# Turning a residual during attention: three generator steps for each block of x instead of two

## The chip, the core and the metric

The kernel runs on one core of a Trainium2 chip. The metric is the device time of one execution in microseconds, as the median of several runs. TensorE is called PE here, VectorE DVE, ScalarE ACT, GpSimd POOL and SyncE SP.

## What is computed

Two layers of the same kind follow each other. Each normalises x in groups of channels, runs attention with 12 heads of 64 channels over 48 x 48 positions, with relative positions added to the scores, projects the result and adds it to x. Cut to what matters:

```
x = x + attention0(group_norm(x))
x = x + attention1(group_norm(x))

attention(x):                                   # x: 2304 positions, 768 channels
    q, k, v = x @ qkv_w + qkv_b                 # layer 0 adds a low-rank term to q and v
    attn = softmax(q * scale @ k.T + rel_h + rel_w)
    return (attn @ v) @ proj_w + proj_b
```

## The kernel before

**Stages.** A layer runs `group_norm`, `project` (keys and values), `project_q` (queries and relative positions), `attend` and `out_project`. Keys, values, queries and relative positions go through DRAM between the stages. x is kept with channels on the partitions, in six blocks of 384 positions (QB); its residual lies in DRAM in that form, as `residuals`. The last projection puts out rows of positions, so in layer 1 the residual has to be turned from channels by positions to positions by channels (`res_tokens`) ahead of it.

**Attention** (`attend_plain`, L864 to L1082). The work is cut into 30 blocks, one pair of heads and up to 512 queries each (L873): five blocks to a pair, of 512, 512, 512, 512 and 256 queries. I call the last a short block. A block goes through 18 tiles of 128 keys in two batches of nine. For each tile PE makes the scores in PSUM (ps_sc, three buffers), ACT their exponentials (pt, L981), DVE adds these up (L987). The values of a batch (ps_ov) are multiplied one batch later, in `catch_up`. So the end of block n lies in block n+1: its denominators (ps_d, L1013) with their reciprocal (L1021) when the second batch of block n is worked off, then the product for o on DVE (L1025), its bias on ACT (L1026), and the stores of o (f_o, L1030) and of the reciprocals (f_rec, L1032), which POOL issues.

**What sets the order.** Instructions given to `in_order` (L158) keep their order in the program on their engine; all PE work of attention does, and so does everything in `turn`. The others are placed by the framework's planner. Each engine runs its queue from the front: an instruction that waits holds all behind it. SP issues the loads of keys (L899), values (L908), queries (L932) and relative positions (L942, L946). POOL issues the stores and all transfers of `turn`.

**Work beside attention.** `attend` gets a generator, `beside` (L1287), and steps it once at the end of each block but the first, 29 times:

```
                if i > 0:
                    next(beside, None)
```

In layer 0 the generator loads the weights of the projection and adds up their four sums (`sums_of_a`, L401: one DVE addition or subtraction to a step, L412). In layer 1 it first runs `turn`:

```
                if li == 1:
                    yield from turn(residuals[1], res_tokens, p3, bt)
                w_all = p3.tile([P, CT, C], F32, tag="w", name="wproj")
```

`turn` (L1216 to L1241) takes the six blocks of x one by one. For each it loads the block (POOL, L1223), adds the projection's bias with six ACT activations (L1226), transposes squares of 32 x 32 with one DVE instruction (L1231), and stores the result with 24 transfers from POOL (L1238). The tile of a block holds the loaded and the turned half, and there is one buffer for it (tag "w"), which the weights of the projection use too. So each load, and that of the weights (L1293) at the end, waits until the stores before it have landed. A block of x takes two steps: a `yield` stands behind its load, and another behind the third of the six activations. There is none at the end of the loop, so the stores of a block and the load of the next one come in the same step: steps 1 to 12 are used, the weights are loaded at step 13, and their sums follow at steps 14 to 17.

Of the kernel before, what the change touches and what calls it, by code (L numbers as in the profile page):

```python
# [55 lines left out]
def two_layers(tc: tile.TileContext, x, layers, out):  # L56


    nc = tc.nc
    with tc.tile_pool(name="verdict", bufs=1) as vp:  # L60
        bad = vp.tile([1, 1], mybir.dt.int32, tag="bad", name="bad")
        compute(tc, x, layers, out, "f", bad)
        again = nc.values_load(
            bad, min_val=0, max_val=1,
            skip_runtime_bounds_check_because="the result of a comparison",
        )
        with tc.If(again > 0):
            compute(tc, x, layers, out, "g", None)
# [3 lines left out]
def compute(ctx: ExitStack, tc: tile.TileContext, x, layers, out, run, bad):  # L72
# [38 lines left out]
    def scratch(name, shape):  # L111
        name = f"{run}_{name}"
        return dram.tile(shape, F32, tag=name, name=name)
# [44 lines left out]
    def in_order(instruction):  # L158

        tc.keep_in_program_order(instruction)  # L160
# [1055 lines left out]
    def turn(res, to, pool, bt):  # L1216


        for b in range(NQB):

            both = pool.tile([P, 2, CT, QB], F32, tag="w", name=f"x_turned_{b}")
            x, turned = both[:, 0], both[:, 1]
            in_order(nc.gpsimd.dma_start(x, res[b]))  # L1223
            yield
            for t in range(CT):
                in_order(nc.scalar.activation(  # L1226
                    x[:, t], x[:, t], AF.Identity, bias=bt[:, t : t + 1]
                ))
                if t == HP - 1:
                    yield  # L1230
            in_order(nc.vector.transpose(  # L1231
                turned.rearrange("p t q -> p (t q)"), x.rearrange("p t q -> p (t q)")
            ))
            rows = to[ts(b, QB), :].rearrange("(f i) c -> i f c", i=32)
            for t in range(CT):
                for r in range(P // 32):
                    lo = t * P + r * 32
                    in_order(nc.gpsimd.dma_start(  # L1238
                        rows[:, :, lo : lo + 32],
                        turned[ts(r, 32), t].rearrange("p (f j) -> p f j", j=32),  # L1240
                    ))  # L1241

    residuals = [[scratch(f"res{li}_{b}", [P, CT, QB]) for b in range(NQB)] for li in range(2)]
    res_tokens = scratch("res_tokens", [N, C])
# [16 lines left out]
    for li, ly in enumerate(layers):  # L1261
# [21 lines left out]
        with tc.tile_pool(name="p3_w", bufs=1, **REUSE) as p3:  # L1283
# [3 lines left out]
            def beside(li=li, ly=ly, p3=p3, bt=bt, w=w):  # L1287
                in_order(nc.gpsimd.dma_start(bt, ly.proj_bt))
# [3 lines that stand above are left out]
                s = p3.tile([P, 3, HP, HP * P], F32, tag="s", name="wproj_s")  # L1292
                in_order(nc.gpsimd.dma_start(w_all, ly.proj_w.rearrange("(t p) n -> p t n", p=P)))  # L1293
                factors, steps = sums_of_a(
                    matrix_blocks(w_all, HP * P), *(s[:, i] for i in range(3))
                )
                w.update(factors)
                yield
                yield from steps
# [95 lines left out]
```

## Time and profile before

| | us |
|---|---|
| median of 3 runs | 3280.67 |
| lowest and highest run | 3269.58 and 3292.76 |
| the profiled execution | 3272.56 |
| its span, from the first instruction to the last | 3270.8 |
| x_turned <- f_res, one load of x, 1152 KB: issue to landing, median | 5.8 |
| f_res_tokens <- x_turned, one of 24 stores, 48 KB: issue to landing, median | 2.4 |
| wproj <- in_proj_w, the weights' load, 2304 KB: issue to landing, median of both layers | 13.6 |

The profile is of one execution. Its page gives the busy time of each engine and the costliest groups of instructions; the timelines give instructions in order of time. A row of a timeline has the start in us from the span's start, the duration in us of all that it holds, engine, line, operation, tiles (out <- in), shapes, count, and, in brackets, how long the engine was idle before it and what ended that. The median of the runs is 8.1 us above the profiled execution, so sums are made on the profile's span and carried over to the median as a difference.

### The profile page before, as it was taken

Reading aid. Unit: us, or ns where it says so; the run is one execution under the profiler, and the core shown is the slowest. Engines: PE = TensorE matmul, PEld = TensorE weight load, DVE = VectorE, ACT = ScalarE, POOL = GpSimd, SP = SyncE. Lnnn points to the kernel's source line nnn. Section 1 sums busy time; section 2 is a strip of 40 time slices with the busy share of each in tenths; the row PEclk is TensorE's granted clock in tenths of the full one; section 3 lists DMA queues with packets and bytes.
Section 4 is the critical chain, followed back from the end, with each engine's and each line's share of the span. In section 5 each row is a group of like instructions: output and inputs, shape, how many; then the busy total and the mean of one; then the engine's idle time right before and its main releaser. Section 6 shows DMA issues by size and latency. Waiting matters only on the chain. (4 is left out here: it accounts for less than half of the span.)

```text
span 3270.8 us, 50009 instructions
## 1 busy us (share of the span) xinstructions
PE 3209.8 (98%) x19600; PEld 1995.9 (61%) x19600; DVE 2112.6 (65%) x2281; ACT 1450.0 (44%) x1673; POOL 468.4 (14%) x855
## 2 busy tenths in 40 slices
PE   8999999999999999999989999999999999999999
PEld 5555666665656665656555566656666656656555
DVE  8432437777777777777774234576778767777764
ACT  3101436555555555653011024655566555555520
POOL 2144110000000000000012531102223200000000
PEclk9999999999999999999999999999999999999999
DMA  7333388353536262724234335766556463435251
GB/s 267 130 82 74 130 261 219 82 128 78 133 74 142 67 152 64 153 62 160 101 126 145 58 106 197 240 137 145 123 136 149 117 147 79 127 78 135 66 205 59
DMA packets 225155, 419.76 MB, mean 128 GB/s; under 512 B 43616, under 2 KB 111104, under 8 KB 221072
## 3 DMA queue, kind: packets, MB, share of 16 engines
q1 hardware_dynamic: 177712, 255.35, 31.8%
q0 software_dynamic: 47200, 161.12, 16.1%
q8 instruction: 158, 2.59, 0.3%
q14 instruction: 85, 0.70, 0.1%
HBM read 260.35 MB, written 155.97 MB: 127 GB/s over the span
## 5 line engine op out<-in xcount | busy, mean ns | idle before, releaser
L987 DVE TENSOR_TENSOR sum<-sum,pt 128x1024 f32<-128x1024 f32 (+1 forms) x960 | 1071.1, 1116 | 187.9 <-ACT pt L981 97.0
L954 PE MATMUL ps_sc<-q,k 64*128 64x512 f32 (+1 forms) x8640 | 1085.6, 371 | 13.9 <-ACT pt L981 12.3
L981 ACT ACTIVATE pt<-ps_sc 128x1024 f32<-128x1024 f32 (+1 forms) x1080 | 1009.8, 941 | 174.4 <-PE ps_sc L954 89.0
L954 PEld LDWEIGHTS ps_sc<-q,k 64*128 64x128 f32 x8640 | 782.2, 185 | 226.0 <-issue 46.0
L954 PE MATMUL ps_ov<-pt,v 128*64 128x512 f32 (+1 forms) x4320 | 857.7, 551 | 0.0
L954 PEld LDWEIGHTS ps_ov<-pt,v 128*64 128x64 f32 x4320 | 301.2, 137 | 497.6 <-issue 443.3
L954 PE MATMUL ps_sc<-rel,places 64*128 64x512 f32 (+1 forms) x2160 | 413.6, 371 | 1.9 <-DMA rel<-f_r 1.6
L1032 POOL DMA_DIRECT2D f_rec<-rec x120 | 58.5, 492 | 1588.5 <-DVE rec L1021 1587.1
L698 PE MATMUL ps_q<-xT,w_q 128*128 128x384 f32 x864 | 285.1, 488 | 0.7 <-DVE v L587 0.7
L1026 ACT ACTIVATE o<-o,v_bias 128x512 f32<-128x512 f32 (+1 forms) x60 | 40.9, 681 | 459.2 <-DVE o L1025 453.6
L954 PEld LDWEIGHTS ps_sc<-rel,places 64*128 64x128 f32 x2160 | 211.7, 185 | 33.4 <-issue 2.6
L698 PEld LDWEIGHTS ps_q<-xT,w_q 128*128 128x128 f32 x864 | 163.0, 191 | 110.1 <-issue 2.5
L1021 DVE RECIPROCAL rec<-ps_d 128x512 f32<-128x512 f32 (+1 forms) x60 | 181.9, 3031 | 2.5 <-PE ps_d L954 2.5
L601 POOL DMA_DIRECT2D f_v<-v x288 | 137.3, 485 | 106.4 <-DVE v L587 101.5
L987 DVE TENSOR_TENSOR sum<-pt 128x1024 f32<-128x1024 f32 (+1 forms) x60 | 67.0, 1117 | 128.9 <-ACT pt L981 128.9
L523 PE MATMUL ps_k<-xt,w_k 128*128 128x384 f32 x432 | 145.1, 492 | 3.6 <-DVE xt L427 2.6
L704 DVE TENSOR_SCALAR x_q<-ps_q,bt 128x384 f32<-128x384 f32 x72 | 44.3, 617 | 159.5 <-PE ps_q L698 159.5
L996 ACT CAST sum<-sum 128x1024 bf16<-128x1024 f32 (+1 forms) x60 | 57.6, 960 | 168.1 <-DVE sum L987 168.1
L523 PEld LDWEIGHTS ps_k<-xt,w_k 128*128 128x128 f32 x432 | 82.3, 192 | 63.9 <-issue 3.6
L523 PE MATMUL ps_k<-xT,w_k 128*128 128x384 f32 x324 | 114.6, 507 | 4.7 <-DVE xT L249 4.6
L999 DVE TENSOR_TENSOR sum<-sum,sum 128x1024 bf16<-128x1024 f32 (+1 forms) x60 | 67.1, 1119 | 61.6 <-ACT sum L998 61.6
L997 DVE TENSOR_TENSOR sum<-sum,sum 128x1024 f32<-128x1024 f32 (+1 forms) x60 | 67.1, 1119 | 61.6 <-ACT sum L996 61.6
(183 smaller groups left out, 2474.7 us busy)
## 6 DMA issues: line engine op xcount, KB each, us to landing
rel<-f_r SPq DMA_DIRECT2D x1152, 96.0 KB, 4.3
f_k<-xs POOLq DMA_DIRECT2D x72, 384.0 KB, 2.9
f_q<-xs_q POOLq DMA_DIRECT2D x48, 576.0 KB, 3.8
k<-f_k SPq DMA_DIRECT2D x48, 576.0 KB, 5.2
q<-f_q SPq DMA_DIRECT2D x96, 256.0 KB, 3.2
f_r<-relh POOLq DMA_DIRECT2D x48, 432.0 KB, 5.0
f_r<-relw POOLq DMA_DIRECT2D x8, 2592.0 KB, 18.1
f_v<-v POOLq DMA_DIRECT2D x288, 48.0 KB, 2.0
```

The lines of the kernel that those rows point to most:

```text
L523: nc.tensor.matmul(ps, lhsT=x, rhs=y, start=(t == 0), stop=(t == HP - 1))
L601: nc.gpsimd.dma_start(vd[to : to + KG, :], v[ts(r, KG), k])
L698: nc.tensor.matmul(ps, lhsT=w[:, t, ts(pr, P)], rhs=xT[b][:, t, :], start=(t == 0), stop=(t == CT - 1),)
L704: nc.vector.tensor_scalar(x[:, pr], ps, weights.bt[:, pair : pair + 1], ly.q_scale, ALU.add, ALU.mult,)
L954: in_order(nc.tensor.matmul(*args, **kwargs))
L981: nc.scalar.activation(pt, ps[:, :, 0 : self.n], AF.Exp)
L987: nc.vector.tensor_add(self.sum, self.first if kt == 1 else self.sum, pt)
L996: nc.scalar.copy(hi, self.sum)
L997: nc.vector.tensor_sub(self.sum, self.sum, hi)
L999: nc.vector.tensor_sub(lo, self.sum, mid)
L1021: nc.vector.reciprocal(self.rec, ps)
L1032: nc.gpsimd.dma_start(recs[li][2 * self.pair + r : 2 * self.pair + r + 1, to], self.rec[r * HD : r * HD + 1, :],)
```

## The change

A `yield` is put at the end of the loop over the blocks of x in `turn`:

```diff
@@ -1239,6 +1239,7 @@
                         rows[:, :, lo : lo + 32],
                         turned[ts(r, 32), t].rearrange("p (f j) -> p f j", j=32),
                     ))
+            yield
 
     residuals = [[scratch(f"res{li}_{b}", [P, CT, QB]) for b in range(NQB)] for li in range(2)]
     res_tokens = scratch("res_tokens", [N, C])
```

A block of x now takes three steps: its load; three of its six activations; and the other three, the transpose and the stores. The load of the next block is the step after that. With b from 0 to 5 these are steps 3b+1, 3b+2 and 3b+3. The weights' load becomes step 19, and their sums steps 20 to 23. No instruction is added or left out, and layer 0 doesn't run `turn`. A second version of the computation in the same program (`attend_shifted`), which runs only if a value is out of bounds, runs the generator through at once.

## The prediction

> **What bounds the kernel now.** I read the page first, for the engine that sets the time, then each stage of the second layer's attention by the busy times of chosen windows, then the timelines of the engines in the stages that are too long.
>
> ```profile
> span 3270.8 us, 50009 instructions
> PE 3209.8 (98%) x19600; PEld 1995.9 (61%) x19600; DVE 2112.6 (65%) x2281; ACT 1450.0 (44%) x1673; POOL 468.4 (14%) x855
> ```
>
> TensorE (PE) sets the time: whatever does not stop it costs nothing. The turn of x runs on ACT, DVE and POOL, so its price is only the time in which PE stands still because of it. The windows show where (start and end, length, PE busy; PEclk is the granted TensorE clock):
>
> ```profile
> core 0: us, PE busy (x) PEld busy (x) DVE busy (x) ACT busy (x) POOL busy (x), PEclk, DMA share, GB/s
> 2252.00:2288.00 36.00, 31.88 (x276) 21.55 (x274) 22.95 (x26) 17.83 (x26) 15.42 (x26) 0.95 0.89 230
> 2428.00:2458.00 30.00, 29.57 (x266) 19.60 (x266) 22.16 (x23) 17.22 (x26) 6.49 (x12) 1.00 0.62 172
> 2628.00:2671.00 43.00, 35.12 (x260) 24.75 (x262) 34.01 (x29) 20.73 (x21) 1.56 (x3) 0.92 0.78 153
> 2671.00:2778.00 107.00, 107.00 (x771) 62.88 (x772) 79.81 (x64) 59.78 (x63) 4.65 (x9) 1.00 0.34 76
> ```
>
> PE is idle for 4.1, 0.4 and 7.9 us in three places, and the clock is below 1.00 in two of them; in the last row, after the turn, it never stops. To price the places I measure from the first denominator matmul (ps_d) of one block to that of the next, in PE's timeline. Without a disturbance a pair of heads has the intervals 37.47, 37.47, 32.49, 28.95 and 33.32 us (every pair of layer 0, and the last of layer 1). I number layer 1's blocks from 0; blocks 4, 9, 14, ... are the short ones (256 queries). Interval n runs from ps_d of block n to that of block n+1. Longer than they should be are: interval 3, 35.04 (6.09 too many); 8 and 9, 29.63 and 33.74 (0.68 and 0.42); 14, 43.05 (9.73). Together 16.9 us: this is all that the turn and the load of the weights cost, and all that can be won.
>
> **The first place** (PE, then ACT, then POOL):
>
> ```profile
> 2274.34 0.41 PE L954 MATMUL ps_sc<-rel,places 64*128 64x512 f32 x2
> 2278.82 2.07 PE L954 MATMUL ps_sc<-q,k 64*128 64x512 f32 x8 [4.07 <-ACT pt L981]
> 2280.69 0.63 PE L954 MATMUL ps_sc<-rel,places 64*128 64x512 f32 x2
> 2281.12 1.49 PE L954 MATMUL ps_sc<-q,k 64*128 64x512 f32 x8
> ```
> ```profile
> 2271.41 0.62 ACT L998 CAST sum<-sum 128x512 bf16<-128x512 f32 x1 [0.76 <-DVE sum L997]
> 2276.23 1.62 ACT L1226 ACTIVATE x_turned<-x_turned,bproj 128x384 f32<-128x384 f32 x3 [4.21 <-DMA x_turned<-f_res]
> ```
> ```profile
> 2257.05 9.72 POOL L1238 DMA_DIRECT2D f_res_tokens<-x_turned  x16 [1.47 <-DMA f_res_tokens<-x_turned]
> 2266.76 0.57 POOL L1030 DMA_DIRECT2D f_o<-o  x1
> 2267.33 0.99 POOL L1032 DMA_DIRECT2D f_rec<-rec  x2
> 2268.79 0.57 POOL L1223 DMA_DIRECT2D x_turned<-f_res  x1 [0.47 <-issue]
> ```
>
> Read from below: POOL issues the 24 stores of x block 0 into short block 4, and the load of x block 1, which takes the same buffer, leaves only at 2268.79. It lands 7.1 us later. Block 4 lasts too short: ACT comes to the bias of x block 1 at 2272.0 and waits 4.21 us. Behind it in ACT's queue stand the exponentials of block 5, so the three PSUM buffers of the scores stay full and PE stops for 4.07 us. Then 8 score matmuls take 2.07 us instead of 1.09: the slow clock is the other 2.02 of the 6.09 (0.05 of the window's 36 us is 1.8).
>
> **The second place** (DVE, ACT, PE):
>
> ```profile
> 2628.81 1.36 DVE L412 TENSOR_TENSOR wproj_s<-wproj 128x1152 f32<-128x1152 f32 x1 [9.46 <-DMA wproj<-in_proj_w_dram]
> ```
> ```profile
> 2642.39 0.51 ACT L1026 ACTIVATE o<-o,v_bias 128x256 f32<-128x256 f32 x1 [13.29 <-DVE o L1025]
> ```
> ```profile
> 2643.86 2.08 PE L954 MATMUL ps_sc<-q,k 64*128 64x512 f32 x8 [7.88 <-ACT pt L981]
> ```
>
> The same pattern: the stores of x block 5 go into short block 14, the load of the projection's weights leaves behind them at 2616.35 and takes 12.4 us. DVE wants to add two blocks of them at 2619.35, and waits 9.46 us with the sums and the product for o queued behind; ACT's bias of o waits for that product, with the exponentials behind it, and PE stands for 7.88 us. With the slow clock after it: 9.73.
>
> **The change, part by part.** The generator is stepped once at the end of each block from block 1 on. Before, step 2b+2 is the first half of the bias of x block b, and step 2b+3 is the second half, the transpose, the 24 stores and the next load. Now step 3b+2 is the first half, 3b+3 ends with the stores, and 3b+4 is the next load. Nothing is added to any engine: the same 36 biases, 6 transposes, 144 stores and 6 loads. [...]
>
> The load itself hardly moves: at short block 4 it was already put behind the f_o and f_rec of block 3, and waits for the same stores. What moves is its reader, one block later.
>
> 1. Bias of x block 1: from the end of block 4 (2272.0) to the end of block 5, 33.3 us on (the length of a pair's first block). The load landed at 2275.9, so it is 29 us early. Interval 3 falls to 28.95: **-6.09**.
> 2. Sum of the weights: from the end of block 14 to the end of block 20. The stores of x block 5 now go into short block 19, which is as short as 14, so I put the weight load as far from its start as before: landing some 11.4 us into block 20, 24 us before DVE asks (2.0 us after that block's 33.3). Interval 14 falls to 33.32: **-9.73**.
> 3. Step 9, after a short block, is second half and transpose as before (now of x block 2): its 1.10 us stay, **0**.
> 4. Step 14, after a short block, is now the first half of the bias of x block 4. The trace has no such step there without a wait. From below it costs 0, from above the 1.63 us of its three activations; the nearest row is step 9, the same three activations at the same place, 1.10 us. I take **+1.1**. Its load doesn't wait: x block 1 was loaded 18.1 us after its stores began (2314.04 to 2332.15) and a load takes 5.8 (median of the page), while step 14 comes some 58 us after the stores of step 12 begin.
> 5. All other steps lie at the ends of long blocks, or go into short ones (3, 8, 13 before; 3, 8, 18, 23 now). Their cover is the slack of ACT and DVE beside PE: 37.47 and 32.49 us with them as without. **0**; without that cover 1.6 us for a half bias and 2.6 for a transpose.
> 6. Queues: POOL has f_rec and f_o behind each set of stores as before (14.6 us), and intervals 5 and 7, where that was so, are not longer. On SP nothing is moved, but PE now comes earlier to what SP loads while the stores and the weights take the DMA engines. In block 15, whose place block 20 takes, the second half of the keys landed at 2620.7 and the values at 2630.7. With no stop PE wants them at 2632.0 and 2642.5 (block begun at 2617.4, 10.55 us per batch of scores, 4.04 for values): 11 us to spare for each. **0**.
>
> Sum: -6.09 - 9.73 + 1.1 = -14.7 us on a span of 3270.8: 3256.1. The profiled execution took 3272.6, 8.1 below the median of the runs (3280.67); on that median the sum gives **3266.0**.
>
> **A rule against it.** The Trainium skill, "DMA: Bandwidth & Descriptors", section "Anatomy of one DMA — SWDGE (gpsimd) path", fits a GpSimd-issued transfer as 2.0 us and its bytes at 436 GB/s. That is 4.7 us for the x load (1.18 MB) and 7.4 for the weights (2.36 MB), estimates from that page. The rows say 7.1 and 12.4, beside a DMA share of 0.78 to 0.89. By the rule ACT would wait 1.5 us and DVE 4.4, PE some 1.4 and 2.8, with at most the slow clock of now (2.0 and 1.9): 4.2 to 8.1 us to win, less the 1.1 of item 4, so 3273.7 to 3277.6. I take the rows, since they are the transfers in question.
>
> **Rivals.** *Both waits go* (0.72): 3266.0; for it speaks that both rows name their transfer as the releaser. *Only the first goes* (0.13): the weights' transfer, with SP's loads behind it in block 20, holds PE there as it did in block 15; against it stand the 11 us. -6.1 + 1.1: 3275.7. *Nothing comes of it* (0.09): the planner puts the readers where they were, or the run-to-run spread (3269.6 to 3292.8) is made of other things that grow: 3280.7. *Slower* (0.06): the planner, which places instructions outside the kept order itself, puts SP's loads of keys and queries later once the steps have moved, and PE waits at block boundaries. One such stop costs 6.1 to 9.7 us, as the two above; with two or three of them the gain is gone, and with eight (8 x 6.1 - 14.7 = +34) it is slower by 1%. Nothing in the trace shows such a wait: PE's largest stop for a DMA in this stage is 0.6 us.
>
> **Range and chances.** The likeliest case with the spread of the runs (-11 and +12) gives 3255 to 3278. Below, the fastest run less all 16.9 is 3253; above, the case of no gain is 3281. I say 3250 to 3284. 1%, about what a measurement of this kernel can tell from no change, is 33 us, about twice all that can be won here. Faster by that takes a lucky set of runs, 0.05; slower takes half of the last case, 0.03; within 1%, 0.92.
>
> **What would show it.** Right: no bias of x_turned that waits for its load, no sum of the weights that waits for theirs, intervals 3 and 14 at 28.95 and 33.32 us, interval 13 and 14 together up by about 1, PEclk 1.00 throughout. Wrong: a new stop in block 15 or 20, or ps_sc released by a DMA.

## The result, and the profile after

The changed kernel takes 3258.02 us (median of 13 runs, 3255.04 to 3263.06), the kernel before 3279.15 (13 runs, 3269.58 to 3292.76). The ratio is 0.9935, with a 95% interval of 0.9925 to 0.9946: 21.1 us less, where 14.7 were forecast. The predicted 3266.0 is 8.0 us too high, the range of 3250 to 3284 holds the result, and 0.65% lies within the 1% to which 0.92 was given. The interval is 0.2% wide: these runs tell far smaller differences apart than the 1% that I took for the limit.

The page of the changed kernel, the two lines that were shown of before:

```profile
span 3253.3 us, 50008 instructions
PE 3204.2 (98%) x19600; PEld 1990.3 (61%) x19600; DVE 2112.3 (65%) x2281; ACT 1450.7 (45%) x1673; POOL 470.1 (14%) x855
```

The span is 17.5 us shorter, and PE's busy time only 5.6: the rest was idle time. The windows, in the same columns as before, are laid over intervals 3, 8, 14, 15 to 17, and 18 with 19, where the weights are loaded now (the first is as long as its counterpart before, and so takes in the start of interval 4):

```profile
2250.00:2286.00 36.00, 35.95 (x330) 24.07 (x328) 27.39 (x29) 18.23 (x26) 16.53 (x29) 1.00 0.87 226
2420.00:2450.00 30.00, 29.92 (x274) 20.02 (x272) 22.40 (x24) 17.58 (x26) 7.09 (x13) 1.00 0.58 176
2620.00:2653.00 33.00, 33.00 (x258) 22.00 (x258) 27.53 (x23) 21.90 (x25) 7.24 (x13) 1.00 0.79 160
2653.00:2761.00 108.00, 108.00 (x780) 63.32 (x778) 80.14 (x63) 63.72 (x71) 15.02 (x27) 1.00 0.39 94
2760.00:2824.00 64.00, 63.95 (x540) 44.82 (x538) 49.55 (x48) 38.50 (x45) 18.06 (x30) 1.00 0.90 208
```

In the 36 us of the first row PE stands still for 0.05 us, in the 30 us of the second for 0.08, and the clock is 1.00 in all five, though the DMA engines are as busy as before (0.87 where it was 0.89). ACT's timeline at the first place, then POOL's:

```profile
2269.61 0.62 ACT L998 CAST sum<-sum 128x512 bf16<-128x512 f32 x1 [0.76 <-DVE sum L997]
2270.55 1.03 ACT L981 ACTIVATE pt<-ps_sc 128x1024 f32<-128x1024 f32 x1 [0.32 <-PE ps_sc L954]
...
2301.75 1.62 ACT L1226 ACTIVATE x_turned<-x_turned,bproj 128x384 f32<-128x384 f32 x3
```
```profile
2266.90 0.57 POOL L1223 DMA_DIRECT2D x_turned<-f_res  x1 [0.48 <-issue]
```

The load of x block 1 leaves at the same place as before; ACT goes from the cast straight to the exponentials, and the bias comes 31 us later and waits for nothing. At the second place, POOL's load of the weights and DVE's first sum:

```profile
2781.87 0.90 POOL L1294 DMA_DIRECT2D wproj<-in_proj_w_dram  x1 [4.15 <-DMA f_res_tokens<-x_turned]
```
```profile
2812.03 1.23 DVE L999 TENSOR_TENSOR sum<-sum,sum 128x1024 bf16<-128x1024 f32 x1 [1.11 <-ACT sum L998]
...
2813.17 1.35 DVE L412 TENSOR_TENSOR wproj_s<-wproj 128x1152 f32<-128x1152 f32 x1
```

No idle time stands ahead of L412. Measured again from ps_d to ps_d, the intervals of layer 1 in the changed kernel are 29.04 (interval 3), 29.28 and 33.72 (8 and 9), 29.28 (13) and 33.31 us (14); the rest are those of an undisturbed pair. What the turn still costs is 1.1 us.

### The profile page after: what moved, and what is told of

Its sections match the earlier page's. It is cut to its first block, busy times and chain, and to the rows that moved or that the text cites. A ratio compares the mean times of both kernels' runs of the same rounds, so it can differ in the third digit from the quotient of the medians.

```text
span 3253.3 us, 50008 instructions
## 1 busy us (share of the span) xinstructions
PE 3204.2 (98%) x19600; PEld 1990.3 (61%) x19600; DVE 2112.3 (65%) x2281; ACT 1450.7 (45%) x1673; POOL 470.1 (14%) x855
## 4 chain that ended last, share of the span: by engine, by line
PE 81%; issue 12%; POOL 2%; DMA 2%; DVE 1%; SPq 1%; ACT 1%; POOLq 0%; DVEq 0%; ACTq 0%
PE ps_sc L954 34%; PE ps_ov L954 25%; PE ps_v L523 7%; PE ps_q L698 4%; PE ps_k L523 4%; PE psy L1186 4%; PE ps_d L954 1%; PE psr L637 1%; DMA f_r<-relw 1%; POOL f_k L567 1%; POOL f_q L630 1%; DMA flat<-in_relh_t_dram 0%; POOL f_r L663 0%; PE psc L637 0%; ACT pt L981 0%
## 6 DMA issues: line engine op xcount, KB each, us to landing
f_r<-relw POOLq DMA_DIRECT2D x8, 2592.0 KB, 18.1
```

## Experiments

All times of before are medians of runs on the same chip as the experiment. Each experiment changes `turn`, or the generator around it, and computes the same.

**Only the weights later** (from the kernel before):

```diff
@@ turn, at the end of the loop
+            if b == NQB - 1:
+                yield
```

> The turn as before, two steps to a block of x; one more step between the last stores and the load of the weights, so that their first sum comes at the end of long block 15 and not of short block 14. Theory (each wait costs by itself, by where its reader stands): the wait of DVE for the weights is gone, interval 14 falls from 43.05 to 33.3 us, interval 3 stays at 35 or so with its wait of 4 us on ACT; the profiled span is 9.7 us below that of before, 3261, and the median some 10 to 13 us below before. Rival (what counts is that the turn's transfers are spread over more blocks): the turn is spread as before, so no more than 2 us are gained. Rival (the run-to-run spread of before lies in the two waits): the spread of the runs narrows to about half.

Measured: 3261.84 us (5 runs, 3260.17 to 3265.26) against 3280.32; ratio 0.9947 (0.9934 to 0.996), 18.5 us less. Interval 14 is 33.32 and interval 3 is 34.94, with PE's stop for x as before:

```profile
2271.73 0.41 PE L954 MATMUL ps_sc<-rel,places 64*128 64x512 f32 x2
2275.97 2.03 PE L954 MATMUL ps_sc<-q,k 64*128 64x512 f32 x8 [3.83 <-ACT pt L981]
```

The stores go into the same blocks as before and the weights leave at about the same place (2615.71); only the sums come a block later. So the rival of the thinner spread falls. The gain has the predicted place, but it is 18.5 us and not 10 to 13: the wait for the weights, 9.73 us in the first profile, is worth more in the runs. The runs lie within 5.1 us of each other, 27 of before within 10.6; five runs are too few to settle the rival on the spread.

**The kernel before, profiled again** (three times; the second and the third time for one execution each):

> The kernel before, unchanged, for a second profile of it and its spread. Theory (the runs of before differ because the two transfers take longer in some): the profiled execution, if it is nearer the median of 3279 than the first profile (3272.6), shows longer waits at the two places, by about what its span is longer, and intervals elsewhere the same within 1 us. Rival (the spread is spread over the whole kernel): the two waits are as in the first profile, 4.2 and 9.5 us, and the rest of the span is longer. Ratio 1.000 within 0.002.

> The kernel before, unchanged, for a third profile. Theory (which of two loads leaves first sets the wait for the weights): if POOL's load of the weights in short block 14 leaves after SP's load of the values, it takes 15 to 17.5 us, DVE waits 14 us or more, interval 14 is 48 to 50 us and the execution takes 3277 or more; if it leaves first, 12 to 13 us, a wait of 9 to 10, interval 14 at 43 and 3270 to 3274. Rival (the landing varies by chance): no such link.

> The kernel before, unchanged, for a fourth profile. The same link as for the third: weights after values, 15 to 17.5 us and an interval 14 of 48 to 50; weights first, 12 to 13 us and 43.

Measured: 3280.28 us (14 runs), ratio to before 1.0004 (0.9995 to 1.0014); the two single executions took 3277.22 and 3278.61. In the first of these profiles (span 3277.9) DVE's wait is:

```profile
2634.67 1.36 DVE L412 TENSOR_TENSOR wproj_s<-wproj 128x1152 f32<-128x1152 f32 x1 [15.20 <-DMA wproj<-in_proj_w_dram]
```

PE stops for 13.62 us behind it:

```profile
2649.72 2.07 PE L954 MATMUL ps_sc<-q,k 64*128 64x512 f32 x8 [13.62 <-ACT pt L981]
```

The four profiles of before, side by side:

| span of the profile, us | weights leave after (+) or ahead of (-) the values | weights: issue to landing | DVE waits | interval 14 | interval 3 |
|---|---|---|---|---|---|
| 3270.8 (the one shown before) | -1.12 | 12.4 | 9.5 | 43.05 | 35.04 |
| 3277.9 | +0.92 | 16.1 | 15.2 | 49.98 | 36.04 |
| 3275.5 | +0.90 | 16.7 | 15.7 | 50.19 | 35.93 |
| 3276.9 | +1.83 | 17.9 | 17.9 | 51.25 | 36.55 |

The second column is read from the issues of POOL and SP (SPq in the rows). The first profile:

```profile
2616.35 0.90 POOL L1293 DMA_DIRECT2D wproj<-in_proj_w_dram  x1 [1.97 <-DMA f_res_tokens<-x_turned]
2617.47 0.37 SPq L908 DMA_DIRECT2D v<-f_v  x1
```

and the second:

```profile
2617.59 0.37 SPq L908 DMA_DIRECT2D v<-f_v  x1
2618.01 1.74 SPq L932 DMA_DIRECT2D q<-f_q  x2
2618.51 0.90 POOL L1293 DMA_DIRECT2D wproj<-in_proj_w_dram  x1 [3.25 <-issue]
```

Where the weights left first, they landed in 12.4 us and the values took 13.2; where the values left first, they landed in 5.3 and the weights took 16.1. In the five other profiles in which this load left just behind the values of a pair (0.5 to 2.6 us) it took 15.3 to 17.5 us: those of the changed kernel, twice, of the weights later, of the x wait taken away and of the wait put back. So the profile on which the prediction was summed was an unusually mild one, and the 7 us by which its interval 14 falls short are nearly the whole of the 7.1 us between its span and that of the second profile. In the two single executions the weights left behind the values, and the intervals of 50.19 and 51.25 are at and a little above the upper end of what was expected. The other half of that expectation, weights first, came in one profile of the four. That the order of the two issues sets the landing is therefore a link in the profiles, not a cause shown; no run set that order by itself.

**The two steps, begun one block later** (from the kernel before):

```diff
@@ beside
                 if li == 1:
+                    yield
                     yield from turn(residuals[1], res_tokens, p3, bt)
```

> The turn as before, two steps to a block of x, but begun one block of queries later. The stores and the next load then go into short block 9 (x block 3) and not into short blocks 4 and 14, and the weights are loaded in long block 15. Theory (a stop comes only where a load waits behind stores in a short block and its reader stands at that block's end): interval 3 falls to 29, interval 14 to 33.3, and a new stop of 4 us or so, with some 2 of slow clock, appears in intervals 8 and 9, where before had 1.1 us; span 9 to 11 us below before. Rival (the spread of transfers decides): same span as before within 2 us. Rival (the third step itself is needed): both old stops stay or move, span as before.

Measured: 3277.11 us (14 runs, 3266.34 to 3280.57), ratio 0.9983 (0.9974 to 0.9992). The stops did move, but I had sized them far too small, and one that I had not expected came with them. ACT at the end of short block 9:

```profile
2455.51 1.62 ACT L1226 ACTIVATE x_turned<-x_turned,bproj 128x384 f32<-128x384 f32 x3 [12.07 <-DMA x_turned<-f_res]
```

PE stops for 12.19 us and interval 8 is 43.73. And DVE at the end of block 15, which I had thought long enough:

```profile
2670.03 1.36 DVE L412 TENSOR_TENSOR wproj_s<-wproj 128x1152 f32<-128x1152 f32 x1 [7.80 <-DMA wproj<-in_proj_w_dram]
```

PE stops for 3.67 us, interval 15 is 43.06 instead of 37.47. Intervals 3 and 14 have only the price of a step there (29.28; 33.75). POOL's timeline shows where both come from. At block 9 (the first of the stores, and the load behind the last):

```profile
2422.09 5.51 POOL L1238 DMA_DIRECT2D f_res_tokens<-x_turned  x9 [19.87 <-DVE x_turned L1231]
...
2444.51 0.57 POOL L1223 DMA_DIRECT2D x_turned<-f_res  x1 [3.98 <-DMA f_res_tokens<-x_turned]
```

The stores' issues are drawn out and the load behind them waits for their landing, so that it leaves 22.4 us after the first store, and then takes 10.7 us. At block 4 of the kernel before these were 18.1 and 7.1 us; the two differences make 7.9 us, by which ACT waits longer (12.07 for 4.21). At block 15 the weights leave 19.7 us after the first store and take 16.8. Why the same transfers take longer here than at block 4 stays open. (The weights' 16.8 us came 9 us behind the nearest load of values, with queries and relative positions beside it: the values are not the only load that can hold it up.) A step holding both stores and load therefore needed more than a pair's first block (33.3 us) ahead of the reader when the load was the weights', and not only more than a short block. These are the waits of one execution of 3278.59 us; three of the 14 runs took under 3270, so the stops need not be as long in all of them.

**The three steps, begun two blocks later** (from the changed kernel):

```diff
@@ beside
                 if li == 1:
+                    yield
+                    yield
                     yield from turn(residuals[1], res_tokens, p3, bt)
```

> The changed kernel, three steps to a block of x, begun two blocks of queries later, so that the stores go into short block 9 and the weights are loaded in the middle of a pair. Theory (with the load a step behind the stores no phase has a stop): as the changed kernel within 1.5 us, span 3253 to 3256, no wait of ACT for x or of DVE for the weights; 21 us below the median of before. The load of the weights, with SP's loads of keys and values not beside it, lands in 9 to 12 us and not 17.3. Rival (the phase of the change is what helped): a stop of 4 us or more in interval 8 or 9 or 13 or 14.

Measured: 3256.24 us (5 runs), ratio 0.9933 (0.992 to 0.9945); no wait of ACT for x, none of DVE for the weights, no interval more than 0.45 us too long. Two loads of x took 11.0 and 11.1 us here, as long as the one that stopped PE in the experiment before, and nothing waited for them: with the load a step behind the stores neither this phase nor that of the change has a stop. The weights, loaded in block 21 with no change of pair beside them, landed in 9.0 us. With the weights later and the x wait left in, 3261.84 us on the same chip, the difference is 5.6 us, and the interval 3 of that kernel was 5.99 too long: about so much the x wait is worth once the weights' is gone.

**Only the x wait taken away** (from the kernel before; the weights as they were):

```diff
@@ turn
             in_order(nc.gpsimd.dma_start(x, res[b]))
             yield
+            if b == 1:
+                yield
...
-                if t == HP - 1:
+                if t == HP - 1 and b != 1:
                     yield
```

> The turn as before, two steps to a block of x, but all six activations of x block 1 come together at the end of long block 5 and none at the end of short block 4; the weights as before. Theory (the two waits are separate and add up): no wait of ACT for x, interval 3 at 29 us instead of 35 to 36; the wait of DVE for the weights stays, 9 to 16 us, interval 14 at 43 to 50; six activations at once (3.2 us) at the end of a long block cost under 1 us; median 5 to 7 us below before, and with the 18.5 of the weights alone it makes up the 21 to 24 of the change. The spread of the runs stays as wide as that of before. Rival (the two overlap or one pushes the other about): the median is within 2 us of before, or 10 us and more below.

Measured: 3274.32 us (11 runs, 3269.87 to 3277.91) against 3278.34; ratio 0.9986 (0.9976 to 0.9995): 4.0 us less. Interval 3 is 29.06, interval 14 stays at 48.76. But interval 9 is 38.59, with a third stop of PE at the end of block 10:

```profile
2478.62 1.62 ACT L1228 ACTIVATE x_turned<-x_turned,bproj 128x384 f32<-128x384 f32 x3 [3.90 <-DMA f_rec<-rec]
```
```profile
2481.21 1.37 PE L954 MATMUL ps_sc<-q,k 64*128 64x512 f32 x8 [3.03 <-ACT pt L981]
```

The row names another DMA, but this is the bias of x block 4, whose load landed at 2478.36, after 11.4 us, where it took 5.7 in the first profile. There it had landed with 4 us to spare. The two-step turn so has a third place that is nearly late. Interval 9 is 4.85 us above the 33.74 of the first profile, so the 4.0 us of the medians are what the removed wait gave less what the new stop took, if that comes in the other runs too. The expectation of 5 to 7 us is missed, and this run can't say whether the two waits add up; the 18.5 us of the weights and the 5.6 left for x are steps of one chain to the 24.1 of the three steps begun two blocks later, and no second test of it. The spread of the runs is 8 us here and 17 in before, though the weights' wait is still there; where the spread of before lies I can't say.

**The weights' wait put back** (into the changed kernel):

```diff
@@ beside
                 w.update(factors)
-                yield
+                if li == 0:
+                    yield
                 yield from steps
```

> The changed kernel, but the first sum of the weights comes in the same step as their load, at the end of short block 19: the wait for the weights is put back, at another place and with nothing else altered. Theory: DVE is ready some 2 us into block 20 and waits for a landing that the changed kernel had 20 us into it, so 16 to 18 us; PE stops for 1.6 us less (14 to 16.5) and some 2 us of slow clock follow; span 16 to 18.5 us above that of the changed kernel, 3270 to 3272, median 4 to 6 us below before. Rival (DVE's wait reaches PE only in part, since ACT has its own queue): less than 8 us.

Measured: 3274.98 us (12 runs) against 3278.34, ratio 0.9988 (0.998 to 0.9997), and 17.9 above the changed kernel on the same chip. DVE's and PE's rows:

```profile
2798.39 1.36 DVE L412 TENSOR_TENSOR wproj_s<-wproj 128x1152 f32<-128x1152 f32 x1 [17.75 <-DMA wproj<-in_proj_w_dram]
```
```profile
2813.43 2.08 PE L954 MATMUL ps_sc<-q,k 64*128 64x512 f32 x8 [16.16 <-ACT pt L981]
```

Interval 19 is 51.85 instead of 33.32, 18.5 us more. One wait of DVE, put back at another place with the three steps kept (all four sums come one step sooner), takes away five sixths of the gain.

**No step at the end of a short block** (from the changed kernel):

```diff
@@ turn
                 if t == HP - 1:
                     yield
+                    if b in (2, 5):
+                        yield
```

> The changed kernel with an empty step where a step of the turn fell to the end of short block 9 or 19, so that no half bias and no transpose stands between a short block and a long one. Theory (what is left of the turn's cost stands at these ends alone): intervals 8, 9, 13 at 28.95 and 33.32 us within 0.1; the profiled attention of layer 1 1.1 us shorter than in the changed kernel; the medians can't be told apart. Rival (the rest is DMA contention): the intervals stay 0.3 us too long.

Measured: 3256.47 us (5 runs, 3253.12 to 3257.68), ratio to before 0.9928 (0.9914 to 0.9941). Intervals 8, 9 and 13 are 28.95, 33.32 and 28.95, and from the first to the last ps_d layer 1 takes 978.2 us instead of the 979.3 of the changed kernel. The turn is then free: its last microsecond was the work of ACT between a short block and a long one, though only the profile can tell this version from the changed kernel.

**The changed kernel again:**

> The changed kernel, unchanged, on the same chip as the three others: the measure for them, and a second profile. No wait for x or the weights; the landing of the weights again some 17 us after the issue, 12 to 15 us ahead of the sum; 20 to 24 us below before, runs within 8 us of each other.

Measured: 3257.11 us (5 runs, 3254.84 to 3259.53), ratio 0.9934 (0.992 to 0.9947). The weights landed in 17.4 us, and no wait for x or for them is there.

## Why the prediction was right, and which term was too small

**The mechanism** held at both places: each is a reader that stands at the head of its engine's queue before its load has landed, with the exponentials behind it in ACT's own queue (first place) or behind ACT's bias of o, which waits for DVE (second place). The removal of the weights' wait alone, the wait that was put back, and interval 3 with the x wait alone removed show it, not only the profile of the change.

**Item 1** (bias of x block 1, -6.09): interval 3 went from 35.04 in the first profile, and 35.93 to 36.55 in the others, to 29.04: 6.0 to 7.5 us. The expected 29 us to spare were 28 (load landed at 2273.9, bias at 2301.75).

**Item 2** (first sum of the weights, -9.73) is the term that was mis-sized. Its interval goes to 33.31 as forecast, but in three of the four profiles of before it comes from 50 to 51 and not from 43.05: 16.7 us between the second profile of before and the changed kernel, and 18.5 in the medians when it alone is removed. The step at fault is the carrying over: "8.1 below the median of the runs (3280.67); on that median the sum gives 3266.0". It takes the 8.1 us for something outside the sum, and most of them were in the very term that I was pricing. The cover was smaller than I said, too: I put the landing 11.4 us into block 20 and 24 us ahead of DVE; it came 19.9 us into it (PE began the block at 2779.2, the load landed at 2799.1), 14 us ahead.

**Items 3 and 4**: step 9 went from 1.10 to 0.73 us, where I had put no change, and step 14, for which I took 1.1, costs 0.33. The nearest row held two things that the first half of the bias has not. One is DVE's idle time of 0.46 us before the last addition of short block 9, in front of the step: it stands in all six profiles with the two-step turn in its old phase and not in the changed kernel, delays ACT by 0.35 us, and what causes it stays open. The other is the transpose behind the step: the same three activations cost 0.3 us without it and 0.7 with it (in the changed kernel, and so too at three such steps of the one begun two blocks later). In item 4 the load at 2332.15 is that of x block 2, behind the stores of x block 1; the 58 us came out (bias of x block 4 at 2610.35, stores from 2551.62).

**Items 5 and 6**: no other interval changed, and SP's loads came in time in block 20. (A pair's fourth interval of 28.95 us does not hold for the last pair, where it is 22.19 in both layers, before and after alike; nothing was summed on it.)

**The sum**, with what the second profile of before shows: -7.0 (interval 3), -16.7 (14), -0.35 (8 and 9) and +0.3 (13), so -23.7, of 24.6 between the spans of those two profiles and 21.1 between the medians. With the first profile the same sum is -15.8 of 17.5; the other 1.7 lie ahead of layer 1's first block, in work that the change doesn't touch. The gap between the spans is wider than that between the medians mostly because the profiled execution of the changed kernel (3255.04 us) is 3.0 us below its own median. That the result lies in the stated range is owed to the spread of the runs of before, which was added on both sides, more than to the sum.

**The rule against it** (the fit in the Trainium skill, "DMA: Bandwidth & Descriptors", section "Anatomy of one DMA — SWDGE (gpsimd) path") would have made less of the change than the rows, 4.2 to 8.1 us before item 4. Block 21, with no change of pair, gave it its best chance: 9.0 and 9.4 us for the weights in the two versions that load them there, where the estimate from the fit is 7.4; the quickest load of x took 5.2, where it is 4.7. At a pair's start the weights take 12.4 to 17.9. The measurement decides, and it says that the rows of one execution were still too kind.

**The rivals.** That only the first wait goes is refuted by interval 14; the weights did meet SP's loads in block 20, where PE did not stop. No mishap of the planner came: SP issues its loads in the same order in both kernels.

## What to carry to other kernels

An instruction placed by hand beside a bound engine should stand behind its load by the load's worst landing in that stage, counted from the stores that the load itself waits for; where blocks differ in length, count it for the shortest. When one profiled execution is well off the median, look for the difference in the wait to be priced, and take a second profile before carrying its size over; here one profile said 9.5 us and three others 15.2 to 17.9. A step that is free at the end of a long block may cost at the end of a short one.

## What the runs showed of the hardware

**A stop costs more than its length.** DVE's wait of 9.46, 15.20 and 17.75 us stopped PE for 7.88, 13.62 and 16.16: 1.58 or 1.59 us less each time. (At the end of long block 15, in the two steps begun later, 7.80 us of DVE stopped PE for only 3.67.) But the interval grew by 9.73, 16.66 and 18.53. The rest, 1.9 to 3.0 us, goes with a slower clock afterwards: eight score matmuls take 2.07 us instead of 1.09. How long the clock stays low differs from stop to stop and not by the stop's length alone. Behind the 7.88 us it was 0.58 for 4 us and then 1.00, behind the 13.62 us 0.50 and then 0.76, which makes an estimated 1.7 and 3.0 us; a stop of 16.29 us, in the last profile of before, cost only 1.6 on top. The slow clock came after a stop of only 3.03 us too (the two stretches from the PE row shown with that stop on), and not after one of 0.38 (last row, from the first profile of before):

```profile
2480.00:2484.00 4.00, 2.79 (x16) 2.27 (x18) 1.79 (x2) 3.87 (x5) 0.00 (x0) 0.75 0.86 186
2484.00:2488.00 4.00, 4.00 (x32) 3.16 (x30) 3.46 (x4) 2.43 (x4) 0.00 (x0) 0.82 0.93 145
2448.00:2452.00 4.00, 3.62 (x32) 2.67 (x30) 2.96 (x2) 4.00 (x7) 0.00 (x0) 1.00 1.05 313
```

**The order in which two large loads left goes with how long they took.** In one profile the weights' load left 1.1 us ahead of the values and took 12.4 us; in three it left 0.9 to 1.8 us behind them and took 3.7 to 5.5 us more, while the values took some 8 us less. With one profile of the first kind, and no run that set the order, this is not shown to be the cause.
